# A local-attention transformer on one core: softmax over whole banks, and three moves in a software pipeline

## The chip, the cores and the metric

The kernel runs on one core of a Trainium2 chip. A core has a matmul engine (PE, with a part that loads weights, PEld), a vector engine (DVE), an activation engine (ACT), a general engine (POOL) and an engine that here only starts transfers (SP). Each works through its own queue of instructions in order and waits on semaphores for what other engines produce. PE writes only into PSUM, which has eight banks of 128 x 512 floats; DVE and ACT can read it[...]. The metric is the device time of one launch in microseconds; the kernel before takes 4255.5 us, the median of three runs (4248.83 to 4255.69).

## The reference, cut to what matters

Two blocks transform 16 sequences of 256 tokens of width 128. The first block is a linear-attention layer, then a local transformer of six layers, which is most of the work; the second is an attention layer and a feed-forward layer. The change lies in the local transformer alone:

```python
# each of 6 layers; x: (16, 256, 128), 16 heads of 64, windows of 32 tokens
x = attn_layer(shift_tokens(x), ...) + x
x = ffn_layer(shift_tokens(x), ...) + x

# attn_layer: q, k, v from x @ Wqkv; q and k normalized, scaled, rotated;
# a window of 32 queries sees its own window of keys and the one before: 64 keys
sim = einsum('bhwie,bhwje->bhwij', bq, bk2) * 8.0
sim = where(mask, -max, sim)
attn = softmax(sim, -1)
out = einsum('bhwij,bhwje->bhwie', attn, bv2)      # then @ Wo

# ffn_layer: layer norm, then a * gelu(gate) @ W2 + b2, with 341 hidden columns
```

## The kernel before, in words

The sequences are taken in eight units of two (512 tokens). A layer has eight pairs of heads; a step handles two pairs of one unit, so a layer has 8 x 4 = 32 steps and six layers 192. The steps run as one software pipeline: in the loop's turn n, different pieces belong to different earlier steps (n - 1, n - 3, n - 4, n - 5, n - 8, n - 9). Inside the local transformer the order of instructions on PE, DVE, ACT and POOL is exactly the order in which the program issues them (`manual_schedule`); only SP's transfers are placed by a planner.

One turn n of the loop issues, in this order:

1. `scaled`: POOL multiplies the keys of step n - 4 by their inverse norms (L837).
2. `merging`: PE multiplies the weighted state of a quarter unit by the merged value and output matrices (L969). After the fourth quarter DVE adds the result to the state (L982).
3. In odd turns `norms_rows`: PE turns the keys' inverse norms (L816), ACT copies them (L818), SP sends them out and back as rows.
4. A call of `go_on(behind)`, which lets the feed-forward part advance by one piece.
5. `rotate`: POOL adds the rotated halves to the queries and keys of step n - 1 (L756, four instructions).
6. `flipped`, first half: PE transposes the attention weights of step n - 5 (L930), and ACT copies them to SBUF (prT). In odd turns `windows`: PE transposes eight windows of the state, which is both keys' and values' input here (L847), ACT and DVE copy one half each (xw), and SP duplicates the result. Then `masked` puts the mask into two banks (L863), and `flipped` does the second half, copied by DVE (L936).
7. In even turns `norms_sum`: PE sums squares for the norms (L764), ACT copies the sums (L773).
8. `weighted`: PE multiplies windows and attention weights (L948); ACT and DVE copy the results (L963, L961). Another `go_on`.
9. `scores`: PE multiplies queries and keys of step n - 4 (L885) on top of the mask, into two banks `sims[par]`; then `maxima` on DVE (L897, and L899 for nb, the maximum times minus the inverse norm).
10. In even turns `norms_inverse`: PE transposes the sums of squares (L782), DVE makes a first guess of the inverse root (L784 for nx, L793 for ny), and POOL takes three of Newton's steps (L800 to L808). The result rn is what the softmax scales its logits with. Another `go_on`.
11. `project`, four times (queries and keys of two pairs of heads): PE (L740), the square on ACT (L743), two products with the rotation tables on DVE (L745, L748), and transfers on SP that swap halves (L750, L751). A last `go_on` stands after the first two. The softmax of step n - 4 is woven in: `exponentials` is a generator that the projections pull forward, and each pull emits two exps on ACT.
12. `divided`: the reciprocal of the sums on DVE (L920), the product on POOL (L922), once for each half.

The exps work on 64 columns at a time, since the maximum and the scale differ for each block of 64 keys and an ACT instruction takes one bias and one scale for each partition: 16 in a step, each with an accumulator output for its sum, which is a second instruction in the profile.

The feed-forward part `ffn` is a generator too: it starts in a turn divisible by four, before the third `go_on`, and every `yield` ends one piece. Its pieces are the mean (L995, L997), the squares (L1000), the variance (L1004 on PE, L1012 on DVE, L1014 and L1016 on POOL), the normalized state (L1021, L1022, L1023), the gates (L1031 on PE, L1033 the gelu on ACT), the a part (L1041 on PE, L1045 on DVE) and the output (L1054, L984).

All matrix results but the scores and the layer's sum go through `bank()`, a tag with four buffers that are given out in turn; a buffer is free again when all its readers are done:

```python
pss = psum(es, 4, 3)          # four banks of tag mm, three of tag sim
def bank():
    return stage["ps"].tile([128, 512], F32, tag="mm", name="mm")
```

Of the kernel before, what the change touches and what calls it, by code (L numbers as in the profile page):

```python
# [13 lines left out]
AF = mybir.ActivationFunctionType  # L14
ALU = mybir.AluOpType
AX = mybir.AxisListType
# [3 lines left out]
NU = B // 2  # L20
U = 2 * L
DEPTH = 6
# [22 lines left out]
def adaln_kernel(  # L45
# [5 lines left out]
    nc = tc.nc  # L51
# [27 lines left out]
    def small(tag, shape, bufs=4):  # L79
        return (stage.get("small") or sm).tile(list(shape), F32, tag=tag, name=tag, bufs=bufs)  # L80
# [199 lines left out]
    with block:  # L280
# [19 lines left out]
        pt = bank()  # L300
# [341 lines left out]
    with ExitStack() as es:  # L642
# [111 lines left out]
        def rotate(m, q, got):  # L754
            for j, r in enumerate((q, ks[m % 8][:, :, PAD:])):
                nc.gpsimd.tensor_tensor(r, r, two(got[:, j, :]), ALU.add)  # L756
# [82 lines left out]
        def windows(u, s):  # L839


            xw = atile("xw", (128, 8, 128))
            for g in range(2):
                pt = bank()
                for j in range(4):
                    w0 = 32 * (4 * g + j)
                    nc.tensor.transpose(  # L847
                        pt[0:64, j * 128 : (j + 1) * 128], zs[u][:, s, w0 : w0 + 64], ident
                    )
                dst = xw[0:64, 4 * g : 4 * g + 4, :].rearrange("p w d -> p (w d)")  # L850
                if g:
                    nc.vector.tensor_copy(dst, pt[0:64, :])
                else:
                    nc.scalar.copy(dst, pt[0:64, :])
            nc.sync.dma_start(xw[64:128], xw[0:64])
            return xw

# [33 lines left out]
                                skip_group_check=True,  # L891
                            )

        def maxima(sim, rn):

            mx = small("mx", (128, 8))
            nc.vector.tensor_reduce(mx, sim.rearrange("p (b k) -> p b k", b=8), AX.X, ALU.max)  # L897
            nb = small("nb", (128, 8))
            nc.vector.scalar_tensor_tensor(nb, mx, -1.0, rn, ALU.mult, ALU.mult)  # L899
            return nb  # L900

        def exponentials(x, sims, nbs, rn, pr, ssum):

            for par in range(2):
                for st in range(4):
                    b = 4 * x + st
                    nc.scalar.activation(  # L907
                        pr[:, x, st, par, :],
                        sims[par][:, b * 64 : (b + 1) * 64],
                        AF.Exp,  # L910
                        bias=nbs[par][:, b : b + 1],
                        scale=rn[:, par, b : b + 1],
                        accum_out=ssum[:, x, st, par : par + 1],
                    )
                    if st % 2:
                        yield

        def divided(pr, ssum):
            rsum = small("rsum", (128, 8))
            nc.vector.reciprocal(rsum, ssum.rearrange("p t h -> p (t h)"))  # L920
            prf = pr.rearrange("p t h k -> p (t h) k")
            nc.gpsimd.tensor_tensor(  # L922
                prf, prf, rsum.unsqueeze(2).to_broadcast([128, 8, 64]), ALU.mult
            )

        def flipped(p, x, pr, prT):

            pt = bank()
            for st in range(4):
                nc.tensor.transpose(  # L930
                    pt[:, st * 128 : (st + 1) * 128],
                    pr[:, x, st].rearrange("p h k -> p (h k)"),
                    ident,
                )
            if x:
                nc.vector.tensor_copy(prT[:, p + x, :], pt)  # L936
            else:
                nc.scalar.copy(prT[:, p + x, :], pt)

        def weighted(j, xw, prT):  # L940

# [48 lines left out]
        def ffn(u, i):  # L990
# [37 lines left out]
            for c, n in enumerate(FFC):  # L1028
# [3 lines left out]
                gt = ftile("fg", bufs=3)  # L1032
                nc.scalar.activation(gt[0:n, :], pg[0:n, :], AF.Gelu, bias=bcol(i, f"g{c}", n))  # L1033
                gates.append(gt)
            yield
            yield
            yield
            yield
            for c, n in enumerate(FFC):
                pa = bank()  # L1040
                nc.tensor.matmul(  # L1041
# [3 lines left out]
                nc.vector.scalar_tensor_tensor(  # L1045
                    gt, pa[0:n, :], bcol(i, f"a{c}", n), gt, ALU.add, ALU.mult
                )
            yield
            yield
            yield  # L1050
            yield
            py = bank()
            for c, n in enumerate(FFC):
                nc.tensor.matmul(  # L1054
# [9 lines left out]
        QS = NP // 2  # L1064
# [6 lines left out]
        xws, zxs, pys = {}, {}, {}  # L1071
# [4 lines left out]
        def place(n):  # L1076

            return n // per, n % per // QS, 2 * (n % QS)
# [12 lines left out]
        n = 0  # L1091
        while n < N + 9 or behind:
# [18 lines left out]
            if 0 <= n - 1 < N:  # L1111
                for m in (2 * (n - 1), 2 * (n - 1) + 1):
                    rotate(m, qs[m], got.pop(m))
            if 0 <= n - 5 < N:
                i, u, p = place(n - 5)
                if p == 0:
                    prTs[i, u] = atile("prT", (128, NP, 512))
                flipped(p, 0, prs[n - 5], prTs[i, u])
            for s, lag in ((0, 7), (1, 9)):
                v, r = divmod(n - lag, QS)  # L1120
                if r == 0 and 0 <= v < DEPTH * NU:
                    xws[v, s] = windows(v % NU, s)
# [6 lines left out]
            v, r = divmod(n - 8, QS)  # L1129
# [15 lines left out]
            go_on(behind)  # L1145
            between = exponentials(0, sims, nbs, rn, pr, ssum) if sims else iter(())
            for m in (2 * n, 2 * n + 1):
                if n < N:
                    i, u, p = place(n)
# [1 line left out]
                if m % 2 == 0:  # L1151
                    go_on(behind)
            if sims:
                for x in range(2):
                    for _ in between:
                        pass
                    divided(pr[:, x], ssum[:, x])
                    between = exponentials(1, sims, nbs, rn, pr, ssum) if x == 0 else iter(())
# [33 lines left out]
    with ExitStack() as es:  # L1192
# [23 lines left out]
        for p in range(NP):  # L1216
            bias = wc.tile([128, 2, 384], F32, tag=f"bias{p}", name=f"bias{p}")
# [181 lines left out]
        n = 0  # L1399
        while n < N + 3 or running or merging:  # L1400
# [3 lines left out]
            if merging:  # L1404
                u, p = merging.pop(0)
# [16 lines left out]
            if 0 <= n - 2 < N:  # L1422
                u, g, s, j = steps[n - 2]
# [5 lines left out]
            if 0 <= n - 3 < N:  # L1429
                u, g, s, j = steps[n - 3]  # L1430
# [116 lines left out]
```

## Time and profile before

| | |
|---|---|
| median of three runs | 4255.5 us |
| the profiled execution's own time | 4254.63 us |
| its span, first to last instruction | 4252.8 us |
| local transformer, first to last L897 | 308.4 to 3573.5 us |
| PE, PEld busy | 3979.4 us (94%), 2576.8 us (61%) |
| DVE, ACT, POOL busy | 2826.8 (66%), 2839.5 (67%), 2619.5 us (62%) |
| mean granted clock of PE | 0.983 of full speed |
| exps and their accumulator reads (L907) | 1229.5 + 773.9 us |
| maxima (L897), nb (L899) | 263.2 + 156.1 us |
| division on POOL (L922, 128 x 512) | 398.3 us |

A row of a group gives the line, the engine, the operation, output and inputs by the program's names, the shape and the count; behind the first bar stand the busy time in us and the mean of one instruction in ns, behind the second the time for which the engine stood idle just before, and who released it. In a view in order of time the first number is the start in us from the begin of the span, the second the time until the last of the instructions in the row has ended. A float matmul shows as two instructions. Matmuls overlap in the pipeline, so a busy PE is not a PE at its peak.

### The profile page before, as it was taken

Reading aid. Unit: us, or ns where it says so; the run is one execution under the profiler, and the core shown is the slowest. Engines: PE = TensorE matmul, PEld = TensorE weight load, DVE = VectorE, ACT = ScalarE, POOL = GpSimd, SP = SyncE. Lnnn points to the kernel's source line nnn. Section 1 sums busy time; section 2 is a strip of 40 time slices with the busy share of each in tenths; the row PEclk is TensorE's granted clock in tenths of the full one; section 3 lists DMA queues with packets and bytes.
Section 4 is the critical chain, followed back from the end, with each engine's and each line's share of the span. In section 5 each row is a group of like instructions: output and inputs, shape, how many; then the busy total and the mean of one; then the engine's idle time right before and its main releaser. Section 6 shows DMA issues by size and latency. Waiting matters only on the chain.

```text
span 4252.8 us, 118394 instructions
## 1 busy us (share of the span) xinstructions
PE 3979.4 (94%) x45491; PEld 2576.8 (61%) x45491; DVE 2826.8 (66%) x6003; ACT 2839.5 (67%) x9800; POOL 2619.5 (62%) x3326
## 2 busy tenths in 40 slices
PE   7867999999999999999999999999999998899998
PEld 4534666666666666666666666666666666454544
DVE  6746667777676777667676767776676765455554
ACT  4535666766767666666766666766667665578785
POOL 5446666676666776676766677666767673343432
PEclk9889999999999999999999999999999999999999
DMA  1334344444444444444444444444444441100000
GB/s 40 40 95 106 100 108 102 113 103 106 109 100 113 106 108 104 106 115 104 104 107 104 114 101 109 106 105 113 105 104 100 108 102 58 46 3 6 4 6 6
DMA packets 193548, 371.06 MB, mean 87 GB/s; under 512 B 42538, under 2 KB 83417, under 8 KB 192985
## 3 DMA queue, kind: packets, MB, share of 16 engines
q1 hardware_dynamic: 192984, 363.50, 34.2%
q8 instruction: 360, 5.90, 0.6%
q14 instruction: 204, 1.66, 0.1%
HBM read 127.92 MB, written 8.91 MB: 32 GB/s over the span
## 4 chain that ended last, share of the span: by engine, by line
PE 45%; DVE 23%; ACT 19%; issue 6%; POOL 5%; DMA 1%; SPq 0%; POOLq 0%; DVEq 0%; ACTq 0%
ACT pr L907 10%; PE mm L948 9%; PE sim L885 7%; DVE sent L745 6%; PE mm L764 4%; ACT sq L743 4%; PE mm L930 4%; POOL pr L922 4%; DVE k L748 3%; DVE q L748 3%; PE mm L740 3%; DVE mx L897 2%; PE mm L847 2%; PE mm L1334 2%; DVE nb L899 2%
## 5 line engine op out<-in xcount | busy, mean ns | idle before, releaser
L907 ACT ACTIVATE pr<-sim,nb,rq 128x64 f32<-128x64 f32 x3072 | 1229.5, 451 | 336.9 <-DVE nb L899 328.9
L922 POOL TENSOR_TENSOR pr<-pr,rsum 128x512 f32<-128x512 f32 x384 | 398.3, 1042 | 809.9 <-DVE rsum L920 769.4
L907 ACT ACTIVATION_READ_ACCUMULATOR pr<-sim,nb,rq 128x1 f32 x3072 | 773.9, 252 | 0.0
L969 PEld LDWEIGHTS y<-zx,wvo 128*128 128x128 f32 x6144 | 715.7, 192 | 91.5 <-issue 88.7
L969 PE MATMUL y<-zx,wvo 128*128 128x128 f32 x6144 | 717.5, 275 | 1.3 <-ACT zx L963 1.2
L740 PE MATMUL mm<-z,wqk 128*128 128x512 f32 x1536 | 706.4, 602 | 8.6 <-DMA wqk<-in_L_ffn_Wqkv_dram 6.7
L745 DVE SCALAR_TENSOR_TENSOR sent<-mm,vec,rope 128x512 f32<-128x512 f32 x768 | 570.6, 743 | 118.4 <-ACT sq L743 110.2
L756 POOL TENSOR_TENSOR k<-k,got 128x512 f32<-128x512 f32 x384 | 496.1, 1292 | 0.0
L756 POOL TENSOR_TENSOR q<-q,got 128x512 f32<-128x512 f32 x384 | 487.9, 1271 | 12.7 <-DMA got<-sent 10.6
L837 POOL TENSOR_TENSOR k<-k,kn 128x512 f32<-128x512 f32 x384 | 481.8, 1274 | 19.6 <-DMA kn<-rkh 19.6
L743 ACT ACTIVATE sq<-mm 128x512 f32<-128x512 f32 x768 | 475.0, 618 | 24.0 <-PE mm L740 23.9
L740 PEld LDWEIGHTS mm<-z,wqk 128*128 128x128 f32 x1536 | 278.1, 191 | 323.1 <-issue 237.4
L961 DVE COPY zx<-mm 128x512 f32<-128x512 f32 x384 | 265.6, 692 | 256.7 <-PE mm L948 256.7
L963 ACT COPY zx<-mm 128x512 f32<-128x512 f32 x384 | 225.2, 586 | 287.8 <-PE mm L948 287.8
L1307 POOL TENSOR_TENSOR pr<-pr,rsum 128x256 f32<-128x256 f32 (+1 forms) x256 | 206.1, 826 | 317.3 <-DVE rsum L1305 309.9
L948 PE MATMUL mm<-prT,xw 64*128 64x256 f32 x3072 | 389.5, 390 | 3.4 <-DVE zx L961 2.0
L897 DVE TENSOR_REDUCE mx<-sim 128x8 f32<-128x512 f32 x384 | 263.2, 685 | 176.1 <-PE sim L885 176.1
L948 PEld LDWEIGHTS mm<-prT,xw 64*128 64x128 f32 x3072 | 293.5, 187 | 119.8 <-issue 90.4
L930 PE MATMUL mm<-ident,pr 128*128 128x128 f32 x1536 | 246.2, 284 | 106.5 <-POOL pr L922 76.6
L930 PEld LDWEIGHTS mm<-ident,pr 128*128 128x128 f32 x1536 | 175.4, 143 | 272.3 <-POOL pr L922 243.4
L885 PEld LDWEIGHTS sim<-k,q 64*32 64x32 f32 x24576 | 264.9, 105 | 86.7 <-issue 58.4
L885 PE MATMUL sim<-k,q 64*32 64x64 f32 x24576 | 298.8, 226 | 19.1 <-issue 9.8
(250 smaller groups left out, 6545.2 us busy)
## 6 DMA issues: line engine op xcount, KB each, us to landing
got<-sent SPq DMA_DIRECT2D x1536, 128.0 KB
kn<-rkh SPq DMA_DIRECT2D x768, 128.0 KB
xw<-xw SPq DMA_DIRECT2D x96, 256.0 KB
wqk<-in_L_ffn_Wqkv_dram SPq DMA_DIRECT2D x48, 128.0 KB
bhome<-brow SPq DMA_DIRECT2D x1, 3072.0 KB
wv<-in_L_ffn_Wqkv_dram SPq DMA_DIRECT2D x12, 256.0 KB
wo<-in_L_ffn_Wo_dram SPq DMA_DIRECT2D x12, 256.0 KB
xt<-in_x_dram SPq DMA_DIRECT2D x8, 256.0 KB
```

The costliest lines, as they stand in the source:

```text
L740: nc.tensor.matmul(pp, wqk[:, j, :], xs, start=True, stop=True)
L743: nc.scalar.activation(sq, pp, AF.Square)
L745: nc.vector.scalar_tensor_tensor(two(sent[:, j, :]), two(pp), scale, tab[1], ALU.mult, ALU.mult)
L756: nc.gpsimd.tensor_tensor(r, r, two(got[:, j, :]), ALU.add)
L837: nc.gpsimd.tensor_tensor(k, k, two(kn), ALU.mult)
L885: nc.tensor.matmul(sims[par][32 * c : 32 * c + 32, c0 : c0 + 64], q[r, s, t0 : t0 + 32], k[r, s, t0 : t0 + 64], start=False, stop=True, sk ...
L897: nc.vector.tensor_reduce(mx, sim.rearrange("p (b k) -> p b k", b=8), AX.X, ALU.max)
L907: nc.scalar.activation(pr[:, x, st, par, :], sims[par][:, b * 64 : (b + 1) * 64], AF.Exp, bias=nbs[par][:, b : b + 1], scale=rn[:, par, b ...
L922: nc.gpsimd.tensor_tensor(prf, prf, rsum.unsqueeze(2).to_broadcast([128, 8, 64]), ALU.mult)
L930: nc.tensor.transpose(pt[:, st * 128 : (st + 1) * 128], pr[:, x, st].rearrange("p h k -> p (h k)"), ident,)
L948: nc.tensor.matmul(pz[par][:, w * 256 : (w + 1) * 256], xw[r, (2 * k + w) % 8, :], prT[r, :, 64 * k + 32 * w : 64 * k + 32 * w + 32], star ...
L969: nc.tensor.matmul(py[:, j * 128 : (j + 1) * 128], vo[:, h, :], zx[:, h % 2, h // 2, :], start=(h == 0), stop=(h == 2 * NP - 1), skip_grou ...
```

## The change

Softmax. The generator `exponentials` with its 16 exps goes. `logits` takes the maximum of a bank on DVE, subtracts it on DVE into the tile pr in SBUF, and multiplies by rn on POOL, for each of the two banks. `softmaxed` is pulled by the projections: the first two pulls do nothing, the third emits, ahead of the third projection's square and products, one exp for each bank on ACT, the sums of the exps for each bank on DVE, one reciprocal, and the two divisions on POOL. POOL's order in an even turn is therefore the two products, Newton's steps, the divisions.

Copies. Both halves of the flips and of the windows are copied by ACT.

Moves. `windows` is issued ahead of the first half of the flips instead of behind it. In `ffn` one more `yield` stands ahead of the a part and one less behind it, so the a part moves from the turn's first `go_on` to the second, behind `weighted` and ahead of `scores`; the output piece stays where it was.

```diff
-                if g:
-                    nc.vector.tensor_copy(dst, pt[0:64, :])
-                else:
-                    nc.scalar.copy(dst, pt[0:64, :])
+                nc.scalar.copy(dst, pt[0:64, :])
...
+        def logits(sim, rn, dst):
+
+            sim = sim.rearrange("p (b k) -> p b k", b=8)
             mx = small("mx", (128, 8))
-            nc.vector.tensor_reduce(mx, sim.rearrange("p (b k) -> p b k", b=8), AX.X, ALU.max)
-            nb = small("nb", (128, 8))
-            nc.vector.scalar_tensor_tensor(nb, mx, -1.0, rn, ALU.mult, ALU.mult)
-            return nb
...
+            nc.vector.tensor_reduce(mx, sim, AX.X, ALU.max)
+            nc.vector.tensor_tensor(dst, sim, over_keys(mx), ALU.subtract)
+            nc.gpsimd.tensor_tensor(dst, dst, over_keys(rn), ALU.mult)
+
+        def softmaxed(pr):
+
+            yield
+            yield
             for par in range(2):
...
+                nc.scalar.activation(bank_of(pr, par), bank_of(pr, par), AF.Exp)
+            ssum = small("ssum", (128, 2, 4, 2))
+            for par in range(2):
+                nc.vector.tensor_reduce(
+                    ssum[:, :, :, par].rearrange("p x s -> p (x s)"), bank_of(pr, par), AX.X, ALU.add
+                )
+            rsum = small("rsum", (128, 16))
+            nc.vector.reciprocal(rsum, ssum.rearrange("p x t h -> p (x t h)"))
+            for x in range(2):
+                prf = pr[:, x].rearrange("p t h k -> p (t h) k")
+                nc.gpsimd.tensor_tensor(
+                    prf, prf, over_keys(rsum[:, 8 * x : 8 * x + 8]), ALU.mult
+                )
+            yield
...
-            if x:
-                nc.vector.tensor_copy(prT[:, p + x, :], pt)
-            else:
-                nc.scalar.copy(prT[:, p + x, :], pt)
+            nc.scalar.copy(prT[:, p + x, :], pt)
...
-            yield
-            yield
-            yield
-            yield
+            for _ in range(5):
+                yield
             for c, n in enumerate(FFC):
                 pa = bank()
...
-            yield
-            yield
-            yield
-            yield
+            for _ in range(3):
+                yield
             py = bank()
...
+            for s, lag in ((0, 7), (1, 9)):
+                v, r = divmod(n - lag, QS)
+                if r == 0 and 0 <= v < DEPTH * NU:
+                    xws[v, s] = windows(v % NU, s)
             if 0 <= n - 5 < N:
                 i, u, p = place(n - 5)
                 if p == 0:
                     prTs[i, u] = atile("prT", (128, NP, 512))
                 flipped(p, 0, prs[n - 5], prTs[i, u])
-            for s, lag in ((0, 7), (1, 9)):
-                v, r = divmod(n - lag, QS)
-                if r == 0 and 0 <= v < DEPTH * NU:
-                    xws[v, s] = windows(v % NU, s)
             sims = masked() if 0 <= n - 4 < N else None
...
-                nbs = [maxima(sims[par], rn[:, par]) for par in range(2)]
-                ssum = small("ssum", (128, 2, 4, 2))
+                for par in range(2):
+                    logits(sims[par], rn[:, par], bank_of(pr, par))
...
-            between = exponentials(0, sims, nbs, rn, pr, ssum) if sims else iter(())
+            between = softmaxed(pr) if sims else iter(())
```

More of the change, by code (lines that the diff above doesn't have):

```diff
@@ L892, in scores @@
                             )
-        def maxima(sim, rn):
-            mx = small("mx", (128, 8))
-            nc.vector.tensor_reduce(mx, sim.rearrange("p (b k) -> p b k", b=8), AX.X, ALU.max)
-            nb = small("nb", (128, 8))
-            nc.vector.scalar_tensor_tensor(nb, mx, -1.0, rn, ALU.mult, ALU.mult)
-            return nb
-        def exponentials(x, sims, nbs, rn, pr, ssum):
-            for par in range(2):
[L905 to L915, printed above, removed]
-                        yield
@@ L918, in divided, with bank_of, over_keys @@
[L918 to L924, printed above, removed]
+        def bank_of(pr, par):
+            return pr[:, :, :, par, :].rearrange("p x s k -> p (x s) k")
+        def over_keys(v):
+            return v.unsqueeze(2).to_broadcast([128, 8, 64])
@@ L1047, in ffn @@
                 )
-            yield
-            yield
-            yield
-            yield
+            for _ in range(3):
+                yield
             py = bank()
@@ L1153, in adaln_kernel @@
             if sims:
[L1154 to L1158, printed above, removed]
+                for _ in between:
+                    pass
                 prs[n - 4] = pr
```

## The prediction

> **What bounds the kernel now.** I read the page from the top, then the chain of waits and the engines' order of time inside the local transformer, about 308 to 3573 us, where every edit lies.
>
> ```profile
> PE 3979.4 (94%) x45491; PEld 2576.8 (61%) x45491; DVE 2826.8 (66%) x6003; ACT 2839.5 (67%) x9800; POOL 2619.5 (62%) x3326
> ...
> PE   7867999999999999999999999999999998899998
> ...
> L907 ACT ACTIVATE pr<-sim,nb,rq 128x64 f32<-128x64 f32 x3072 | 1229.5, 451 | 336.9 <-DVE nb L899 328.9
> ...
> L907 ACT ACTIVATION_READ_ACCUMULATOR pr<-sim,nb,rq 128x1 f32 x3072 | 773.9, 252 | 0.0
> ```
>
> PE looks full, yet the chain that ended last gives it only 45%. The program repeats every four steps, named here by n mod 4. Between the first score product (L885) of one step and the next, PE shows where it stands still:
>
> ```profile
> 2061.37 1.95 PE L1041 MATMUL mm<-fx,w 128*128 128x512 f32 x4
> 2063.54 1.06 PE L1041 MATMUL mm<-fx,w 128*85 128x512 f32 x2 [0.22 <-DVE rsum L920]
> 2065.05 0.63 PE L930 MATMUL mm<-ident,pr 128*128 128x128 f32 x4 [0.45 <-ACT rkT L818]
> ...
> 2013.24 0.60 PE L930 MATMUL mm<-ident,pr 128*128 128x128 f32 x4
> 2013.67 0.59 PE L863 MATMUL sim<-maskb,ident 128*128 128x512 bf16 x2
> 2014.55 0.66 PE L930 MATMUL mm<-ident,pr 128*128 128x128 f32 x4 [0.28 <-POOL pr L922]
> ```
>
> A 128x512 product goes every 0.43 us, so four L1041 need 1.72, but the next begins 2.17 later: it waits for a bank. Banks of the tag mm go round by four. Counting the calls of bank() from L782's, the fourth projection holds the first bank, and the third product of L1041 is the next to ask for it: it starts as soon as DVE's last L748 is through. That the banks go strictly round explains this wait and the next one (L930 for the bank of L818), and it carries the sum below. The flip at 2014.55 waits for POOL's division instead. From the scores' end (where PE's next work starts) four steps take 16.82 (step 3: 2003.55 to 2020.37), 15.97 (step 0, to 2036.34), 17.42 (step 1, to 2053.76) and 17.45 (step 2, to 2071.21): 67.66 us. PE's work alone is 63.4, so 4.3 us in each of 48 such periods can be won at most.
>
> **What each edit costs in engine time.** Each step loses 16 activations with 16 accumulator reads on ACT, two L899 (407 ns) and one of two L920 (197) on DVE. Each thing added has a row of its own form. Two exps come in, priced by L1000, 128x512 SBUF to SBUF: 647 ns; two subtractions on DVE, priced by L1022, one PSUM and one SBUF input: 675; two products with rn on POOL, as L922 with the same broadcast: 1042; two sums on DVE, as L500, a reduce of 128x512 in SBUF: 685. One prT copy (691 DVE, 585 ACT) and half an xw copy change engine. Totals: ACT 2840 - 2003 + 248 + 168 = 1250; DVE 2827 - 156 - 38 - 199 + 261 + 263 = 2960; POOL 2620 + 400 = 3020. No engine becomes the bound by its sum; what counts is who is late inside a step.
>
> **The step after the change, from the scores' end (0).** DVE: maximum at 0.09, subtraction 0.80 (a dependent start is 0.71 after, an independent one 0.60: L897 to L899, L997 to L745), maximum 1.40, subtraction 2.11, free at 2.71. POOL has finished rotating by 0.3 in steps 0, 2 and 3 (its last division ends about 10.8 after the previous scores, then 2.47 for L837 and 4.9 for L756), so the first product runs 1.6 to 2.6, the second starts 0.08 after the second subtraction ends, at 2.87, to 3.91. The exps follow to 4.63 (5.4 in step 2, where the 1.28 table load comes first). The sums stand on DVE behind four operations of the first two projections (4 x 0.66), which end at 5.35 or later: the exps hide there. If the products took 1.27, as L756, the exps would end 0.5 later, still hidden. But the third and fourth projection stand behind the sums: 0.60 + 0.70 + 0.12 (L920 to the next start) = 1.42, then 2.72 to the end of the last L748.
>
> Step 3: 2.71 + 2.64 + 1.42 + 2.72 = 9.49. Steps 0 and 2 add nx and ny (0.36), step 0 also L997 (0.60): 10.45 and 9.85. Before, by the trace, these ends were 8.2, 8.6 and 9.5. DVE gets later in all, though ACT no longer holds back its L745.
>
> **The collision.** Each even step has ny (L793) directly behind the second subtraction: it starts 0.60 + 0.25 later, at 2.96, and POOL's second product started at 2.87. Before, POOL was idle there, save once:
>
> ```profile
> 2225.88 1.28 POOL L756 TENSOR_TENSOR k<-k,got 128x512 f32<-128x512 f32 x1
> ...
> 2226.11 1.09 DVE L793 TENSOR_SCALAR ny<-nx 128x64 int32<-128x64 int32 x1
> 2227.12 0.68 DVE L997 TENSOR_TENSOR fx<-z,mm 128x512 f32<-128x512 f32 x1
> ...
> L793 DVE TENSOR_SCALAR ny<-nx x96: 195/195/1091, 283.9 to 3528.6; 128x64 int32<-128x64 int32 x96
> ...
> L899 DVE SCALAR_TENSOR_TENSOR nb<-mx,rq x327: 166/305/1099, 599.7 to 3392.0; 128x8 f32<-128x8 f32 x164
> ```
>
> The three numbers are minimum, median and maximum: 195 ns became 1091 behind a POOL instruction begun 0.23 earlier. L899, with two SBUF inputs, always ended about 1.29 after the start of the L756 it met, so POOL lets go 1.12 after its start, 0.15 before its recorded end; for a product of 1.04 this is 0.89. An offset of 0.10 then costs DVE 0.79. The Trainium skill ("SBUF — State Buffer", Who interferes with whom) says the same of the pair of ports that VectorE and GpSimd share: whichever issues first has it for the whole instruction, and tensor_scalar can need it, tensor_reduce never. By the rule's whole instruction the stall is 0.94, by the rows 0.79; over 96 even steps that is 14 us, and I take the rows. The rule also says the sums are safe. It leaves open who wins at an offset of 0.10: among L899 the nearest are 0.19 behind a POOL start (blocked) and 0.07 ahead (free). One other row lies between, L275 at 3779.32, 0.03 ahead of a POOL start, which took 1.36 instead of 0.48. So I take blocked, nine in ten if my offset holds.
>
> In step 1 L1023 (0.85, of which 0.43 was already such a wait) starts at 3.42 and meets the first product, begun at 3.2, because POOL's 1.66 for L1014 and L1016 makes it late there: it ends at 4.48, and the last L748 at 4.40 + 2.64 + 1.42 + 2.72 = 11.18.
>
> The skill's "GPSIMD Engine Reference" (Engine selection) also speaks against the products on POOL: elementwise belongs on VectorE, about twice as fast. The rows give 1042 against 675, a factor of 1.5. On DVE the two would add 1.2 us to its path and free it of the 0.79 in even steps: 0.4 later in even steps, 1.2 in odd ones. By the rule POOL is the wrong place; by the rows, with DVE setting the end, it is the cheaper one.
>
> **Moves, and the sum.** Windows ahead of the flips (steps 1 and 3) take their two banks in front of the flip's, so in step 1 its second transposition waits for the fourth projection of step 0, and the flip stands behind it. Its DMA on SP (L855) still waits for a copy, and the next transfer in SP's queue, kn, is wanted a step later: nothing. The a part in step 3 goes behind the weighted state: PE's cover ahead of the flip falls from 10.2 to 8.5 there, and the 2.58 stand ahead of the scores. L816 waits for Newton's end (8.5 in step 2, where PE asks at 7.5): hidden by the bank that comes at 9.4. With 0.13 to 0.15 that PE needs to refill after a stall, as before:
>
> Step 0: 11.24 + 0.06, second transposition 0.44, flip and mask 0.86, then 3.86 to the scores' end, 0.13: 16.6, against 15.97 (+0.63). Step 1: 11.18 + 0.08 + 0.87 + 5.62 + 0.13 = 17.88, against 17.42 (+0.46). Step 2: 10.64 + 0.05 + 0.87 + 6.44 + 0.15 = 18.15, against 17.45 (+0.70). Step 3: PE's own 9.59 + 0.86 + 5.62 = 16.07, against 16.82 (-0.75): here division really comes earlier, second half at 9.1 instead of 11.0. Sum +1.04 a period, 48 periods: +50 us. The profiled execution took 4254.6 (span 4252.8), the median is 4255.5: 4305.
>
> **Rivals.** (a) Without the collision: ny passes because the product starts a little later than I read. Steps 0 and 2 lose 0.79 each, POOL is then late enough in step 1 for L1023 to be done at 4.2: steps 15.8, 17.6, 17.4, 16.1 = 66.8, that is -0.8 a period: 4215. It decides once the product starts 0.15 later against ny. (b) One even step collides, or L1023 slips past: the middle, 4255. (c) Exps late: if POOL starts its products 1.5 later than said, the sums hold back the third projection by 0.5 in each step, 2 us a period more: 4400; against it stands POOL's idle time of 353 us before L922 in 1500. (d) PE never waits: 63.7 a period, 190 us less, 4065; for it speak PE's 94% and the shorter wait for division, against it the round of the banks.
>
> **How the numbers follow.** My forecast has 0.62, (a) 0.18, (b) 0.10, (c) 0.07, (d) 0.03. The forecast's own range is 4270 to 4345 (0.5 us a period of misreading each way, a little more above); the range reaches down to (a): 4205 to 4345. 0.2% (8.5 us) is about what a measurement of this kernel can tell from no change. Slower 0.66 (nearly all of the forecast, (c), a third of (b)); same 0.09; faster 0.25.
>
> **What would show it.** Right: L793's median near 1000 ns instead of 195; PE idle before L847 and L930 put down to DVE; ACT near 1250 us busy; POOL's idle before L922 far smaller. Wrong: L793 still at 195; PE's waits at the flips gone; a period below 67.

## The result, and the profile after

The changed kernel takes 4283.7 us (median of four runs, 4280.8 to 4286.4) against 4252.2 us (4248.3 to 4255.7): a ratio of 1.0074, with a 95% interval of 1.0057 to 1.0092, so 31.5 us slower. The forecast was 4305, its range 4205 to 4345. The profiled execution took 4286.4 us, and its span is 4284.6 against 4252.8. From the first to the last step's first maximum, inside the local transformer, it is 3292.8 us (312.25 to 3605.07) against 3264.3, which is 28.5 of the 31.8 us.

The page of the changed kernel (L911 is the exp, L904 the product with rn, L921 the division):

```profile
PE 3991.4 (93%) x45491; PEld 2569.8 (60%) x45491; DVE 3062.5 (71%) x5907; ACT 2098.5 (49%) x4328; POOL 3013.0 (70%) x3710
...
PE 58%; DVE 21%; POOL 7%; issue 7%; ACT 4%; DMA 2%; SPq 1%; DVEq 0%; POOLq 0%; ACTq 0%
...
L921 POOL TENSOR_TENSOR pr<-pr,rsum 128x512 f32<-128x512 f32 x384 | 392.8, 1044 | 317.4 <-DVE rsum L918 313.5
...
L904 POOL TENSOR_TENSOR pr<-pr,rq 128x512 f32<-128x512 f32 x384 | 405.8, 1063 | 220.1 <-DVE pr L903 218.3
...
L911 ACT ACTIVATE pr<-pr 128x512 f32<-128x512 f32 x384 | 231.4, 625 | 154.6 <-POOL pr L904 153.9
```

The chain that ended last (the second line above), as it was before the change:

```profile
PE 45%; DVE 23%; ACT 19%; issue 6%; POOL 5%; DMA 1%; SPq 0%; POOLq 0%; DVEq 0%; ACTq 0%
```

ACT lost 741 us of busy time, and its share of the chain fell from 19% to 4%. Yet the kernel got slower; DVE has nearly kept its share, 21% from 23%. The waits of PE say more. First those of the kernel before (line waited at, releaser, us in all, times, longest):

```profile
PE mm L930 <- POOL pr L922: 76.6, 128, 6.2
PE mm L930 <- ACT rkT L818: 18.2, 40, 0.5
...
PE mm L816 <- POOL rk L807: 11.7, 4, 4.5
...
PE mm L1041 <- DVE rsum L920: 8.1, 37, 0.2
```

and then those of the changed kernel:

```profile
PE mm L816 <- POOL rk L807: 61.1, 52, 4.9
PE mm L740 <- DVE fx L994: 23.0, 45, 0.5
PE mm L930 <- ACT xw L851: 22.1, 81, 0.3
PE mm L1028 <- DVE q L748: 21.5, 40, 0.7
...
PE mm L740 <- DVE fx L1019: 16.4, 45, 0.7
...
PE mm L930 <- POOL pr L921: 14.8, 7, 4.6
```

The wait of the flips (L930) for the division fell from 76.6 to 14.8 us. In its place stand waits for Newton's end (L816) and, in L740 and L1028, for banks that DVE still has to read. Here is step 0 in order of time, PE first, then DVE and POOL. A step is counted from the end of its scores, which is 2044.38 here:

```profile
2045.73 2.86 PE L740 MATMUL mm<-z,wqk 128*128 128x512 f32 x6
2049.10 1.13 PE L740 MATMUL mm<-z,wqk 128*128 128x512 f32 x2 [0.51 <-DVE fx L994]
```

```profile
2046.59 0.69 DVE L903 TENSOR_TENSOR pr<-sim,mx 128x512 f32<-128x512 f32 x1
2047.19 0.21 DVE L784 TENSOR_SCALAR nx<-mm 128x64 f32<-128x64 f32 x1
2047.44 1.01 DVE L793 TENSOR_SCALAR ny<-nx 128x64 int32<-128x64 int32 x1
2048.37 0.68 DVE L994 TENSOR_TENSOR fx<-z,mm 128x512 f32<-128x512 f32 x1
...
2055.09 0.74 DVE L748 SCALAR_TENSOR_TENSOR k<-mm,vec,rope 128x512 f32<-128x512 f32 x1
```

```profile
2047.36 1.04 POOL L904 TENSOR_TENSOR pr<-pr,rq 128x512 f32<-128x512 f32 x1 [0.21 <-DVE pr L903]
2048.53 0.32 POOL L800 TENSOR_TENSOR na<-nx,ny 128x64 f32<-128x64 f32 x1
```

ny (L793) starts 0.08 us behind POOL's second product and takes 1.01 us. L994, which stands behind ny on DVE, is the only reader of the bank that the mean (L992) wrote, and the fourth projection waits 0.51 us for it.

| step | before | forecast | after, these four steps | after, median of 48 |
|---|---|---|---|---|
| 0 | 15.97 | 16.60 | 16.31 | 16.38 |
| 1 | 17.42 | 17.88 | 18.18 | 18.03 |
| 2 | 17.45 | 18.15 | 17.79 | 17.85 |
| 3 | 16.82 | 16.07 | 16.28 | 16.28 |
| sum | 67.66 | 68.70 | 68.56 | 68.54 |

All are us. The last column is the median time from one step's first L902 to the next step's; before the change those medians are 16.11, 17.29, 17.55 and 16.74.

### The profile page after: what moved, and what is told of

Read it like the earlier page. It is cut to its first block, busy times and chain, and to the rows that moved or that the text cites. A ratio compares the mean times of both kernels' runs of the same rounds, so it can differ in the third digit from the quotient of the medians.

```text
span 4284.6 us, 113539 instructions
## 1 busy us (share of the span) xinstructions
PE 3991.4 (93%) x45491; PEld 2569.8 (60%) x45491; DVE 3062.5 (71%) x5907; ACT 2098.5 (49%) x4328; POOL 3013.0 (70%) x3710
## 4 chain that ended last, share of the span: by engine, by line
PE 58%; DVE 21%; POOL 7%; issue 7%; ACT 4%; DMA 2%; SPq 1%; DVEq 0%; POOLq 0%; ACTq 0%
PE mm L945 8%; PE y L966 7%; PE sim L882 6%; PE mm L740 5%; DVE pr L903 4%; PE mm L930 4%; DVE mx L902 4%; PE mm L764 4%; PE mm L1036 3%; PE mm L1047 3%; DVE sent L745 2%; PE sim L860 2%; PE mm L1324 2%; PE sim L1261 2%; ACT pr L1286 1%
## 5 line engine op out<-in xcount | busy, mean ns | idle before, releaser
L740 PE MATMUL mm<-z,wqk 128*128 128x512 f32 x1536 | 738.5, 613 | 46.0 <-DVE fx L994 23.0
L743 ACT ACTIVATE sq<-mm 128x512 f32<-128x512 f32 x768 | 434.6, 591 | 671.6 <-PE mm L740 671.6
L921 POOL TENSOR_TENSOR pr<-pr,rsum 128x512 f32<-128x512 f32 x384 | 392.8, 1044 | 317.4 <-DVE rsum L918 313.5
L904 POOL TENSOR_TENSOR pr<-pr,rq 128x512 f32<-128x512 f32 x384 | 405.8, 1063 | 220.1 <-DVE pr L903 218.3
L740 PEld LDWEIGHTS mm<-z,wqk 128*128 128x128 f32 x1536 | 268.3, 192 | 402.7 <-issue 177.2
L756 POOL TENSOR_TENSOR q<-q,got 128x512 f32<-128x512 f32 x384 | 490.2, 1276 | 26.6 <-DMA got<-sent 15.3
L756 POOL TENSOR_TENSOR k<-k,got 128x512 f32<-128x512 f32 x384 | 489.7, 1275 | 0.0
L902 DVE TENSOR_REDUCE mx<-sim 128x8 f32<-128x512 f32 x384 | 263.6, 686 | 173.5 <-PE sim L882 173.5
L935 ACT COPY prT<-mm 128x512 f32<-128x512 f32 x384 | 224.5, 585 | 296.5 <-PE mm L930 289.8
L945 PEld LDWEIGHTS mm<-prT,xw 64*128 64x128 f32 x3072 | 284.7, 188 | 121.6 <-issue 86.7
L882 PEld LDWEIGHTS sim<-k,q 64*32 64x32 f32 x24576 | 262.1, 105 | 105.8 <-issue 52.3
L882 PE MATMUL sim<-k,q 64*32 64x64 f32 x24576 | 295.6, 226 | 17.6 <-POOL k L837 16.6
L911 ACT ACTIVATE pr<-pr 128x512 f32<-128x512 f32 x384 | 231.4, 625 | 154.6 <-POOL pr L904 153.9
L903 DVE TENSOR_TENSOR pr<-sim,mx 128x512 f32<-128x512 f32 x384 | 265.6, 692 | 27.2 <-POOL k L756 0.5
```

The costliest lines, as they stand in the source:

```text
L740: nc.tensor.matmul(pp, wqk[:, j, :], xs, start=True, stop=True)
L743: nc.scalar.activation(sq, pp, AF.Square)
L882: nc.tensor.matmul(sims[par][32 * c : 32 * c + 32, c0 : c0 + 64], q[r, s, t0 : t0 + 32], k[r, s, t0 : t0 + 64], start=False, stop=True, sk ...
L902: nc.vector.tensor_reduce(mx, sim, AX.X, ALU.max)
L903: nc.vector.tensor_tensor(dst, sim, over_keys(mx), ALU.subtract)
L904: nc.gpsimd.tensor_tensor(dst, dst, over_keys(rn), ALU.mult)
```

## The experiments

Two readings stood against each other. The theory of the forecast: DVE's path sets the end through the banks of the tag mm, and the collision of ny with the product lengthens it. The rival: the banks don't matter, PE waits for POOL's chain (products, Newton's steps, division), and a shorter DVE path gains nothing. Each ratio is against the kernel before, with its 95% interval.

### Softmax alone, moves alone

Softmax alone is the changed kernel with the flips' and windows' second copies on DVE, windows behind the first flip and the a part in its old place:

```diff
-                nc.scalar.copy(dst, pt[0:64, :])
+                if g:
+                    nc.vector.tensor_copy(dst, pt[0:64, :])
+                else:
+                    nc.scalar.copy(dst, pt[0:64, :])
...
-            for _ in range(5):
-                yield
+            yield
+            yield
+            yield
+            yield
```

> The softmax alone, over whole banks; the windows stay behind the flip, the a part ahead of it, and DVE keeps its copies. My theory (DVE later by the sums and by the wait of ny at POOL's port): the whole loss is here and more, since in step 2 the third product of the a part waits for DVE ahead of the flip: 4295 to 4330 us. Rival (the moves are what costs): at most 4260.

Measured: 4300.9 us, 1.0114 (1.0099 to 1.0129), as the theory had it. The new softmax costs about 48 us by itself, and moves and copies together bring 17 of them back. PE waits 61.0 us at L816, 21.9 for the mean's bank and 21.4 at the third gate: the waits of the changed kernel are there without the moves.

Moves alone is the kernel before with windows ahead and the a part later:

```diff
-            yield
-            yield
-            yield
-            yield
+            for _ in range(5):
+                yield
             for c, n in enumerate(FFC):
                 pa = bank()
```

> The two moves alone (windows ahead of the flip, the a part behind the weighted state), with the old softmax and the old copies. My theory: the windows cover 0.8 us of the wait for division in step 0, but in step 2 the division ends about 12 us after the scores, and the 2.6 us of the a part then no longer lie in front of it: some 2 us lost, net +1 us a period, 4290 to 4310. Rival (the moves are harmless or a gain by themselves): at most 4255.

Measured: 4362.2 us, 1.0253 (1.0238 to 1.0268). The direction was right, the size twice what was expected. PE in step 2's turn, the sum of its waits for the division, and its busy time:

```profile
2053.96 0.66 PE L930 MATMUL mm<-ident,pr 128*128 128x128 f32 x4 [1.95 <-POOL pr L922]
2055.49 1.11 PE L930 MATMUL mm<-ident,pr 128*128 128x128 f32 x4 [0.44 <-POOL pr L922]
```

```profile
PE mm L930 <- POOL pr L922: 139.0, 170, 6.2
```

```profile
PE 4040.1 (93%) x45491; PEld 2600.1 (60%) x45491; DVE 2815.6 (65%) x6003; ACT 2834.6 (65%) x9800; POOL 2621.6 (60%) x3326
```

The a part was the cover under which the old softmax's division became ready; without it the flips wait 139.0 us for it instead of 76.6. All in all PE's idle time in the profiled execution grew by 51 us, about what was expected. The other half of the loss is PE's own work: the same 45491 instructions keep it busy for 4040.1 us instead of 3979.4, at a mean granted clock of 0.969 against 0.983. Between 700 and 3300 us the clock records of this run show 23 stretches, nearly all of 3.4 us, at half of the full clock. Each begins within 2 us after the end of one of 33 waits of some 1.9 to 2.0 us at the flips. The kernel before has no such stretch there, and no wait of PE above 1.67 us. So a wait of this length cost PE more than its own time; why the other ten went without, the run does not show.

So the same moves cost 109 us under the old softmax and, with the ACT copies, bring 17 under the new one, whose division is ready earlier: in step 2 it ends 10.7 us after the first maximum by the median, against 12.4 before.

### The collision

A first form issued L782, nx and ny ahead of the scores, where POOL has no product yet:

```diff
             go_on(behind)
+            if n % 2 == 0 and 2 <= n <= N:
+                guess = first_guess(n2)
             if sims:
...
-                rk, inverses[n // 2 - 1] = norms_inverse(n2)
+                rk, inverses[n // 2 - 1] = norms_inverse(*guess)
```

> The changed kernel with the transpositions of the norms and nx, ny ahead of the scores, so that ny is not behind the second subtraction. Collision theory: DVE is 0.8 us earlier in steps 0 and 2, the projection's wait in step 0 (0.9) goes, Newton starts 0.25 earlier for L816 in step 2: -1 us a period, 4225 to 4245. Rival (the longer path of DVE itself is the loss): 4270 or more.

Measured: 4271.8 us, 1.0046 (1.0032 to 1.006), the rival's number. But the edit changes more than ny. PE's L782 now stands ahead of the scores, where it delays all that hangs on them, and there it had to wait for the copies of the weighted state (30.8 us in all). PE's wait for Newton's end rose from 61.1 to 81.1 us.

The next form changes one operand. The Trainium skill ("SBUF — State Buffer", Who interferes with whom) says that a VectorE instruction with at most one SBUF input, outside the modes that use both ports, does not contend with GpSimd, and that tensor_scalar can enter such a mode. L793 is a tensor_scalar with one SBUF input, so by the page it met POOL in such a mode. Here the guess reads the sums from PSUM, where they lie anyway, and has no SBUF input left. Whether that frees it is for the run to show:

```diff
             nc.vector.tensor_scalar(
-                y.bitcast(I32), x.bitcast(I32), -0.5, float(0x5F3759DF), ALU.mult, ALU.add
+                y.rearrange("p (t g e) -> p t g e", t=4, g=4).bitcast(I32),
+                sums.bitcast(I32), -0.5, float(0x5F3759DF), ALU.mult, ALU.add,
             )
```

It leaves out the floor of 1e-24 in the guess; nx, which Newton's steps use, keeps it.

> The changed kernel with one operand exchanged: the first guess (L793) reads the transposed sums from PSUM instead of nx from SBUF[...]; its place, its size and everything else stay. If the collision with POOL's second product is what the 1.0 us of L793 are, its median falls to about 0.2 us, the state-minus-mean (L994) of step 0 is done about 0.8 us earlier, the 0.9 us wait of the fourth projection in step 0 goes, and the time is 4235 to 4265. If DVE's lateness is only a stand-in for POOL's chain (L816 and the flip then wait on POOL for as long), it is 4272 to 4290 with L793 short all the same. If L793 stays near 1.0 us, the reading of the collision was wrong.

Measured: 4231.0 us, 0.9944 (0.9927 to 0.9961), faster than both kernels and 4 us below the theory's range. L793 of the changed kernel and, in this one, the same operation (L788) and L1020 (minimum, median, maximum in ns):

```profile
L793 DVE TENSOR_SCALAR ny<-nx x96: 195/1006/1059, 287.3 to 3562.6; 128x64 int32<-128x64 int32 x96
...
L1020 DVE TENSOR_SCALAR fx<-fx,vec x48: 545/1376/1451, 476.9 to 3661.8; 128x512 f32<-128x512 f32 x48
```

```profile
L788 DVE TENSOR_SCALAR ny<-mm x96: 211/214/216, 284.8 to 3509.2; 128x64 int32<-128x64 int32 x96
...
L1020 DVE TENSOR_SCALAR fx<-fx,vec x48: 545/634/1451, 475.2 to 3607.0; 128x512 f32<-128x512 f32 x48
```

The stall is gone from all 96: the longest guess takes 216 ns. But the edit does two things, since the guess no longer waits for nx either:

```profile
2019.99 0.21 DVE L788 TENSOR_SCALAR ny<-mm 128x64 int32<-128x64 int32 x1
```

```profile
2020.02 1.04 POOL L904 TENSOR_TENSOR pr<-pr,rq 128x512 f32<-128x512 f32 x1 [0.21 <-DVE pr L903]
```

In 90 places it now starts 0.03 us ahead of POOL's product, where it had started 0.08 behind, and there the new order alone could have freed it. Five places settle what the operand does. The second to the sixth guess of both kernels begin 0.15 to 0.60 us inside an L756 of POOL: with the SBUF input they took 724 to 1059 ns, with the one in PSUM 212 to 215.

L1020 in step 1 gained as well, without an edit: there POOL's first product began 2.80 us into the step instead of 3.64, and had nearly let go when L1020 came. So 53 us is what the stalls of both cost, with the 0.12 us for which nx had held up each guess; this run does not part them. Of the waits listed above, that for L994 (23.0) is gone, the one at the third gate fell from 21.5 to 3.6, and L816's from 61.1 to 43.6.

### The banks

One more bank for mm, taken from the three of the scores (sim):

```diff
-        pss = psum(es, 4, 3)
+        pss = psum(es, 5, 2)
```

> The changed kernel with five banks of tag mm and two of tag sim instead of four and three (the scores' banks are free as soon as they are subtracted). If banks are what carries DVE's lateness to PE: the fourth projection's waits in steps 0 and 1 (0.9 and 0.6) and the gates' wait in step 1 (0.7) go, -1.5 to -2 us a period, 4190 to 4215. Rival (the wait is for DVE's data, or only comes back at the flip): 4270 or more.

Measured: 4224.8 us, 0.9934 (0.9919 to 0.9949), 59 us less than the changed kernel, a little above the range of the theory. But for single ones below 1 us, all waits for DVE's banks are gone from PE's list; what is left is POOL:

```profile
PE mm L816 <- POOL rk L807: 81.1, 60, 8.6
PE mm L930 <- POOL pr L921: 27.8, 45, 5.2
```

The same edit in the kernel before:

> The kernel before with five banks of tag mm and two of tag sim. Theory (before, PE waits for the division; the bank waits of step 2 only stand in front of it): 4235 to 4255. Rival (the fifth bank is worth the same 60 us with any softmax, so that it says nothing on the change): 4185 to 4205.

Measured: 4254.1 us, 0.9995 (0.9986 to 1.0003). PE's wait for L818's bank fell there too, from 18.2 to 3.1 us, and the one for L920's is gone. The wait for the division has taken them over:

```profile
PE mm L930 <- POOL pr L922: 125.5, 171, 6.7
```

76.6 became 125.5. Before the change a bank was worth nothing, since POOL's division stood right behind it; after it, it is worth 59 us. The change thus did move the bound, from the division to DVE and the banks, and by the waits of the softmax alone it is the softmax that moved it.

### The products on DVE

```diff
-            nc.gpsimd.tensor_tensor(dst, dst, over_keys(rn), ALU.mult)
+            nc.vector.tensor_tensor(dst, dst, over_keys(rn), ALU.mult)
```

> The changed kernel with the products with rn on DVE instead of POOL. My prediction's term: DVE's path to the projections is 0.4 us longer in even steps (ny no longer meets POOL) and 1.2 in odd ones, more where the product itself, with two SBUF inputs, meets POOL's rotations: 4300 to 4380. By the rule that elementwise work belongs on VectorE, with POOL's chain ahead of the flip 2 us shorter: 4270 or less.

Measured: 4453.8 us, 1.0471 (1.0454 to 1.0489), 170 us more than the changed kernel. ny is back at 196 ns, and still all that stands behind the two products on DVE is late:

```profile
PE mm L740 <- DVE nx L784: 120.7, 90, 2.0
PE mm L740 <- DVE fx L1019: 105.2, 45, 2.5
```

The forecast's working (0.4 us later in each even step, 1.2 in each odd one, so 3.2 a period and 154 us) comes near the 170; the range named for this run was too low for that working. The Trainium skill's table ("GPSIMD Engine Reference", Engine selection) puts elementwise work on VectorE. For the single instruction the trace agrees: 692 ns by the median on DVE, a mean of 1063 on POOL. For its place in this pipeline the table doesn't decide, since DVE is the engine that is late.

### Where L816 stands

L816, the transposition of the keys' inverse norms, waits for Newton's last product. Put behind the second half of the flips:

```diff
                 flipped(p, 1, prs.pop(n - 5), prTs[i, u])
+            if n % 2 and 3 <= n <= N + 1:
+                home = norms_rows(rk)
```

> The changed kernel with L816 (the keys' inverse norms on PE) moved from ahead of the windows to behind the flip's second half. In the changed kernel PE waits 1.05 us there in step 2 for Newton's end. Theory 1 (POOL's chain: product, Newton, division): the flip can't start before the division at 9.9 us, so the wait only moves from L816 to the flip: 4270 to 4285. Theory 2 (L816's place is the loss in step 2): -1 us a period, 4235 to 4250.

Measured: 4454.7 us, 1.0464 (1.0447 to 1.0481): both missed. SP's queue, and POOL at the next product with the keys:

```profile
2001.81 2.42 SPq L828 DMA_DIRECT2D kn<-rkh  x3
2008.60 0.55 SPq L750 DMA_DIRECT2D got<-sent  x1
...
2015.23 6.09 SPq L828 DMA_DIRECT2D kn<-rkh  x5
```

```profile
2018.47 1.27 POOL L837 TENSOR_TENSOR k<-k,kn 128x512 f32<-128x512 f32 x1 [4.39 <-DMA kn<-rkh]
```

Of the four transfers that bring the rows to a step's keys, one now stands in SP's order behind the swaps of the projections (L750, L751), and POOL waits 4.39 us for it. The scores follow (PE waits 60.4 us at L882, 16.6 in the changed kernel), and so does the division (144.8 us at the flips, from 14.8). In the changed kernel the four stand together, ahead of those swaps. A step moved on PE takes its transfers along, and SP's order is laid out anew. Part of the 171 us is the clock, as with the moves alone: PE is busy for 4032.9 us against 3991.4, at a granted clock of 0.971 against 0.980.

### Towards a faster kernel

Five banks with the guess ahead of the scores:

> Five banks and nx, ny ahead of the scores, both on the changed kernel. With five banks what is left is POOL's chain: the waits at L816 (1.2 us in step 2, 0.3 in step 0) and at the flip of step 0 (0.35). Without the collision Newton starts 0.25 earlier in each even step: -0.5 us a period against five banks alone, 4195 to 4210. If the collision still costs DVE's 0.8 on PE's path: 4160 to 4190; if it costs nothing: 4220 to 4230.

Measured: 4274.8 us, 1.0043 (1.0028 to 1.0058): all missed. It is 50 us slower than five banks alone. With the bank waits gone there is nothing to win from a shorter DVE path by this edit, and L782 ahead of the scores only shifts them; PE's wait for Newton's end is 113.5 us against 81.1.

Five banks, with the a part back ahead of the flips (one `yield` fewer ahead of it, one more behind), windows still ahead:

> Five banks, and the a part of the feed-forward back at the turn's first call, ahead of the flips, in step 3's turn; windows stay ahead of the flips. The run with five banks alone took 4224.8. In it the flip behind step 2 starts right at the end of POOL's division and PE stands still ahead of it; with 1.7 to 2.6 us of the a part as cover ahead of the flip, some 0.5 to 1.0 us a period are to be won: 4175 to 4205. If instead the place of the a part behind the weighted state is worth something by itself (it covers the copies of the weighted state ahead of the scores), 4220 to 4240.

Measured: 4179.0 us, 0.9821 (0.9806 to 0.9836), as expected: 46 us less than five banks alone. PE in step 2's turn:

```profile
2033.62 0.28 PE L816 MATMUL mm<-ident,rk 128*32 128x128 f32 x1 [1.00 <-POOL rk L807]
2033.74 2.79 PE L1038 MATMUL mm<-fx,w 128*128 128x512 f32 x6
```

The a part (here L1038) now fills the time before the flips, yet it stands behind L816, which waits 1.00 us. So L816 was put behind it, ahead of windows and flips:

```diff
-            if n % 2 and 3 <= n <= N + 1:
-                home = norms_rows(rk)
             go_on(behind)
             go_on(merges)
+            if n % 2 and 3 <= n <= N + 1:
+                home = norms_rows(rk)
```

> As the kernel beside it (five banks, a part early), and the transposition of the keys' inverse norms (L816) issued behind the two calls that stand ahead of the windows, so behind the a part and the output, but ahead of windows and flips. If the 1.0 us for which L816 waits on Newton's last product is PE's loss in step 2, it goes there: another 0.6 to 1.0 us a period less than the kernel beside it, 4130 to 4180. If the rows' transfer gets late for the product with the keys (as where L816 stood behind the flips, 4454.7), 4300 or more.

Measured: 4152.3 us, 0.9756 (0.9739 to 0.9773), another 27 us. That is in the range, and at 0.56 us a period just under the 0.6 that was the least expected. The rows were not late there. PE's wait for Newton's end fell to 23.3 us; the largest now is:

```profile
PE mm L847 <- DVE k L748: 27.2, 40, 0.8
```

Last, the same with the guess read from PSUM:

> Five banks, the a part early, the keys' rows behind it, and the first guess read from PSUM: the best kernel so far (4152.3) with the collision taken out as well. With four banks taking it out brought 53 us. If the collision costs only while DVE's late products hold PE's banks and the fourth projection, little of that is left to win with a fifth bank, where PE's waits on DVE are nearly gone: 4130 to 4155. If DVE is the clock of the period whatever PE's banks, the whole gain comes again: 4090 to 4115.

Measured: 4111.5 us, 0.966 (0.9644 to 0.9676): 41 us of the 53 came again. The number lies in the second range, that of DVE as the clock of the period whatever PE's banks. The trace doesn't show that cause: step 2 went from a median of 16.86 to 16.11 us, and what left PE's list is the wait at L847 for a bank that DVE had to read. My line on DVE's waits being "nearly gone" overlooked those 27.2 us; the other 14 were not followed. Its page:

```profile
PE 3927.2 (96%) x45491; PEld 2584.0 (63%) x45491; DVE 2952.3 (72%) x5907; ACT 2085.9 (51%) x4328; POOL 3004.4 (73%) x3710
...
PE 80%; DVE 6%; POOL 4%; issue 4%; ACT 4%; DMA 1%; SPq 1%; POOLq 0%; DVEq 0%; ACTq 0%
```

PE now carries 80% of the chain, and four steps take 64.7 us by the median, against the 63.4 that the forecast counted as PE's own work. It is 144 us faster than the kernel before, with the changed kernel's softmax.

## Why the forecast was right, and where not

The direction and the first half of the mechanism were right: DVE gets later, and ny collides with POOL's product. The second half, how this reaches PE, was wrong in the banks, and the total owes part of its nearness to errors that cancel.

**DVE's path.** In step 0 maximum, subtraction, maximum, subtraction were expected at 0.09, 0.80, 1.40 and 2.11 and came at 0.09, 0.88, 1.49 and 2.21; the second product at 2.98 (2.87), ny at 3.06 (2.96). The last L748 ended at 11.45 (11.24 expected) in step 0, 11.76 (11.18) in step 1, 10.85 (10.64) in step 2 and 9.81 (9.49) in step 3. The path was read rightly; each end was put some 0.2 to 0.3 us too early, and 0.6 in step 1.

**The collision.** An offset of 0.08 against 0.10 expected, blocked, 1006 ns by the median against some 985: a stall of 0.81 us, where the rows had said 0.79 and the rule's whole instruction 0.94. The forecast had put 0.79 us on each of 96 even steps into its sum, 76 us, as if every bit of DVE's lateness reached PE, and its rival (a) put 90 us on doing without the stalls. The run with the guess from PSUM gained 53, L1020's part included, so much of the lateness is hidden.

**L1020 in step 1** ended at 4.97 where 4.48 was expected. It was blocked as forecast, but by a product that POOL began at 3.64 and not at 3.2: its rotations ran until then without a pause. This is the term that was too small. (The 0.43 us that the forecast called a wait in L1023 before is 0.31 by its rows: 853 ns by the median less 546 at the least.)

**The banks go strictly round**: this step fell. The forecast made the flips of steps 0, 1 and 2 wait for DVE's last L748. In step 1 the flip began at 2072.18 and in step 2 at 2020.46, while those L748 ended at 2072.45 and 2021.16. And the flip's own wait in the list, for ACT's copy of a window (L851, 81 times), is for a bank that was asked for only one or two calls earlier, since the flip does not read that copy. The buffers are not given out simply in turn. The waits for DVE's banks are real (23.0, 21.5 and 16.4 us, all gone with a fifth bank), but they stand at the fourth projection and the third gate. There they are what a round of four gives for the calls in the program's order, and the forecast's sum had left them out. By what order the buffers are given out over all calls the traces don't tell.

**"L816 is hidden by the bank that comes at 9.4"** fell with it. In step 2 no flip waited for that bank, so Newton's end, forecast for 8.5, was what PE waited for, until 8.7: 61.1 us in all, from 11.7, the largest wait in the list. The forecast's sum for step 2 (18.15) stood 0.3 above what came because its bank wait was longer than the wait that was really there.

**Step 3** gained 0.46 by the median, where 0.75 was expected.

**The sum.** A period was to be 1.04 longer and is 0.90 longer in the four steps shown, 0.85 by the medians; times 48 that would be 41 us against the 28.5 measured. The rest lies in single steps that differ from the median: step 1 once a layer (steps 17, 49, 81, 113, 145) took 18.5 to 18.8 us before and 17.6 to 18.1 after, and four others (7, 15, 123, 159) became 1.7 to 2.2 us shorter, while steps 3, 4, 6 and 8, at the local transformer's start, grew by 1.4 to 3.0. In 3, 4 and 6 PE ran at half of the full clock for 3.4 to 5.0 us longer than before. What else differed in these steps was not followed. So the total came out near the forecast partly by errors of opposite sign: bank waits that weren't there, L816's wait in their place, and irregular steps that gained.

**Engine totals.** POOL 3013.0 (3020). DVE 3062.5 (2960): the difference is ny's 0.81 x 96 and L1020's part of 0.52 x 48 (1376 ns against 853 before), 103 us. ACT 2098.5 against 1250: the two groups of L907, of 1229.5 and 773.9 us, overlap in time with each other and with other rows, and the page counts overlapping time once. By the trace, ACT without L907 was busy for 1686.0 us, so only 1153.5 could be subtracted. It did no harm, as ACT set no end.

**The signs.** Two of the four signs named for "right" came: L793 at 1006 ns by the median, and POOL's idle time before the division, which was

```profile
L922 POOL TENSOR_TENSOR pr<-pr,rsum 128x512 f32<-128x512 f32 x384 | 398.3, 1042 | 809.9 <-DVE rsum L920 769.4
```

before and is 317.4 us after. The two others didn't: ACT is not near 1250 us, and PE's idle time before L847 and the flips is not put down to DVE. One sign of "wrong", PE's waits at the flips gone, came for the most part (76.6 to 14.8).

**The rivals.** "Without the collision, 4215" was a kernel worth building: it runs at 4231.0. One collision only (b) is out: 92 of the 96 L793 took over 900 ns. Late exps (c) are out too: the sums follow the second projection on DVE without a pause (2051.61 in step 0). "PE never waits, 4065" was ruled out for this change, and four edits more come within 47 us of it, at 4111.5.

## What to carry to other kernels

A wait removed is worth no more than the distance to the next one: one more bank was worth nothing with the old softmax and 59 us with the new, and the same moves cost 109 us under the old softmax and, with the copies on ACT, brought 17 under the new. So list PE's waits by releaser again after each edit, and compare its busy time and granted clock too: waits of 1.95 us came with stretches at half clock that nearly doubled the loss. When work moves to POOL, look at what DVE starts within its first tenths of a microsecond; an operand that already lies in PSUM can be read from there, and that one exchange took the stall of 0.8 us out of this loop. Before a step is moved, follow its transfers in SP's order: moving L816 brought 27 us in one place and cost 171 in another, in kernels that differ in the banks and the a part as well.

## What was not expected of the hardware

DVE was held up although its instruction (L1020) had begun 0.05 us ahead of POOL's product by the records (2064.28 against 2064.33). In others of the 48 places it began up to 0.13 us ahead and was held up all the same; it ended 1.32 to 1.34 us after the product's start whether it began 0.13 ahead or 0.55 behind. Who wins is not to be read from recorded starts so close together.

DVE was done sooner than POOL's recorded end allows: ny ended at 2048.45, 0.05 us behind the recorded end of a product of 1.04, though by itself it takes 0.195. Less its own time, POOL would have let go 0.89 us after its start by ny, and 0.79 by L1020 (1.33 less the 0.545 of its shortest case), so the moment is known to some 0.1 us only.
